# A four-layer graph and mixer network on one NeuronCore: the next layer's tables in two halves, and a nine-tap convolution among the experts' tiles

## The chip, the core and the metric

The kernel runs on one NeuronCore of a Trainium2 chip. The core has five engines that run side by side, each its own instruction queue in a fixed order: TensorE (matrix products and transposes, into PSUM, which has eight banks), VectorE, ScalarE, GpSimd and SyncE, which here only issues DMAs. The metric is the device time of one execution in microseconds.

## The reference, cut to what matters

There are 1250 nodes with 512 features and 21250 edges, all in float32. Each of four layers adds a graph convolution and an attention to `x`, and then a mixture of experts. The change touches three of these parts. In layer 0 it is GATv2, three layers in a row:

```python
for k in range(3):
    xl = x @ Wl[k] + bl[k]
    xr = x @ Wr[k] + br[k]
    m = leaky_relu(xl[src2] + xr[dst2] + ea2 @ We[k], 0.2)
    alpha = segment_softmax(m @ att[k], dst2, n)
    out = segment_sum(xl[src2] * alpha[:, None], dst2) + b_out[k]
    x = relu(layernorm(out + x) * gamma[k] + beta[k])
```

In layer 2 it is the graph convolution with four bases and eight heads, and the experts:

```python
agg = segment_sum((x @ W_bases)[src] * norm[:, None], dst).reshape(n, 4, 64)
weightings = (x @ W_comb + b_comb).reshape(n, 8, 4)
out = einsum('nhb,nbf->nhf', weightings, agg).reshape(n, 512) + conv_bias + x @ W_res + b_res
out = relu(layernorm(out) * gamma + beta)
...
logits = conv1d(gelu(conv1d(xt, rc_w1)), rc_w2)      # three taps each, 512 -> 512 -> 10
gates = softmax over the two largest of 10 logits
y = sum over the two chosen experts of gate * (elu(x @ e_w1) @ e_w2)      # 512 -> 256 -> 512
sh = conv1d(silu(conv1d(xt, sh_w1)), sh_w2)          # nine taps 512 -> 256, then one tap 256 -> 512
z = layernorm(x + y + sh) * ln_g + ln_b
```

## The kernel before

The nodes lie in ten tiles of 128 rows (`NT`), the last one partly filled. The program is written with a tile framework: it names buffers by pool and tag, and the framework adds the semaphores and orders each engine's instructions at build time. That order is close to the program's, but it isn't the same: an instruction whose data are expected early may stand before others that were written earlier. Only SyncE's (SP's) order is kept as written in the parts under `manual_schedule`.

**GATv2** (`gat_layer`, L1203). A layer walks over 188 tiles of 128 edges (47 groups of four). For each edge tile TensorE selects the target rows from `hl` with a one-hot matrix (L1280, L1281), VectorE adds the gathered source rows (L1293) and forms the logit as a product with an accumulated sum (L1296). Groups of a block are transposed, exponentiated and mixed (L1347). A finished block of 107 nodes is normed and turned. As soon as a tile of 128 nodes is complete, its part of the next layer's tables is made: `gat_tables` (L1154) returns eight steps, four matmuls for `wl` and four for `wr`. They go into the list `late`, from which the walk takes one step every second edge tile, or every edge tile while more than eight wait (L1486). With the fourth matmul of a product come, in the same step, ScalarE's copy out of PSUM and VectorE's part: for `wl` the product with the attention vector, whose sum is the 513th column (`left`, L1172), for `wr` the rest that the rounded copy leaves (`right`, L1180). Then SP stores the table. PSUM is split 3 `mm`, 2 `tp`, 2 `more`, 1 `tab` here; these products use `tab`.

**Layer 2's graph convolution** (`layer2_attn`, L2484). Per node tile: the residual product, the counts `ct` cast to float (`cs`, L2567 through `evac`), ten matmuls of counts with bases, the scaled sum `ag` (L2577, L2580), four products of a weighting with a basis (L2585, VectorE) that GpSimd adds up (L2588), a layer norm and a ReLU. Steps of the layer's attention stand between (`go`). `evac` (L130) takes ScalarE and VectorE in turn, over all its callers.

**Layer 2's feed-forward part** (`layer2_ffn`, L2600). The norm of `x` goes to `z` and, transposed, to `xp`; three sums and differences of neighbouring columns (`form`, L2687) serve a fast three-tap convolution with four products for two outputs. A filter comes in pieces of three taps (`piece`, L2617): three DMAs and three GpSimd sums. Up to five pieces are held. `conv` (L2639) makes the routing convolution (four filters of one piece), whose output gives the logits; `route` finds the experts and scatters the rows of `z` to the table `routed_in` in memory; then `conv` makes the shared nine-tap convolution (two filters of three pieces, 192 matmuls), and ten second products follow (L2780, L2782), added to `z` (L2783). Only then come the experts.

**The experts** (`experts`, L2311): 29 tiles of 128 routed rows. A tile needs its rows `xe` (256 KB) and its expert's weights `w` (1025 KB), both with four buffers and loaded three tiles ahead by SP. TensorE turns the rows and makes the two products, the activation lies between, and ScalarE's queue stores the output.

Of the kernel before, what the change touches and what calls it, by code (L numbers as in the profile page):

```python
# [12 lines left out]
F32 = mybir.dt.float32  # L13
# [10 lines left out]
N = 1250  # L24
# [33 lines left out]
class Net:  # L58
# [1095 lines left out]
    def gat_tables(self, L, p, t, xT, bank):  # L1154
# [7 lines left out]
        def product(name, c):  # L1162
            def f():
                if c == 0:
                    d[name] = bank()
                nc.tensor.matmul(d[name], lhsT=xT(c), rhs=L[name][:, c, :], start=c == 0,  # L1166
                                 stop=c == 3)
                if c == 3:
                    (left if name == "wl" else right)(d[name])
            return f  # L1170

        def left(m):  # L1172
            o = p.tile([128, D + 1], F32, tag="tlo", name="tlo")
            nc.scalar.copy(o[:, :D], m)
# [5 lines left out]
        def right(m):  # L1180
            o = p.tile([128, 2, D], F32R, tag="tro", name="tro")
            nc.scalar.copy(o[:, 0, :], m)
# [3 lines left out]
        return [product(name, c) for name in ("wl", "wr") for c in range(4)]  # L1186
# [314 lines left out]
    def run(self, fast):  # L1501
# [4 lines left out]
        with self.tc.tile_pool(name="arm", bufs=1) as self.arm:  # L1506
# [23 lines left out]
            with self.psum():  # L1530
# [36 lines left out]
    def gat_first(self, pv, xtab):  # L1567
        nc, I = self.nc, self.I
        L = self.gat_vectors(0, pv)
        with self.tc.tile_pool(name="l0", bufs=1) as p, \  # L1570
# [3 lines left out]
            with self.tc.tile_pool(name="edge", bufs=1, side="right") as pe, \  # L1574
# [19 lines left out]
                def steps():  # L1594
                    for t in range(NT):
                        for i, f in enumerate(self.gat_tables(
# [3 lines left out]
                            if i % 4 == 3:  # L1600
# [710 lines left out]
    def experts(self, table, n, rowI, act):  # L2311
# [5 lines left out]
        with self.tc.tile_pool(name="ex", bufs=2) as p, \  # L2317
                self.tc.manual_schedule(engines={mybir.EngineType.SP}):
            def load(i):
                xe = p.tile([128, D], F32, tag="xe", name="xe", bufs=4)  # L2320
                nc.sync.dma_start(xe, self.rin[i * 128:(i + 1) * 128, :])
                row = nc.sync.value_load(rowI[0:1, i:i + 1], min_val=0, max_val=(n - 1) * 128)
                w = p.tile([128, 2050], F32, tag="w", name="w", bufs=4)
                nc.sync.dma_start(w, table[bass.ds(row, 128), :])
                return xe, w

            ahead = [load(i) for i in range(3)]
            for i in range(ntiles):
                xe, w = ahead.pop(0)
                if i + 3 < ntiles:  # L2330
                    ahead.append(load(i + 3))
# [16 lines left out]
                nc.scalar.dma_start(self.rout[i * 128:(i + 1) * 128, :], o)  # L2348

# [134 lines left out]
    def layer2_attn(self):  # L2484
        nc, I = self.nc, self.I
        added = self.both_added()
        with self.tc.tile_pool(name="l2", bufs=1) as p:
# [17 lines left out]
            with self.tc.tile_pool(name="egc", bufs=2) as tmp, \  # L2505
# [55 lines left out]
                for t in range(NT):  # L2561
# [5 lines left out]
                    self.evac(cs, ct)  # L2567
                    go()
                    y = self.mm([128, parts * 256])
                    for s in range(NT):  # L2570
# [6 lines left out]
                    nc.vector.tensor_scalar(af, y[:, :256], dinv[:, t:t + 1], None,  # L2577
                                            op0=ALU.mult)
# [4 lines left out]
                    for b in range(4):  # L2583
                        m = tmp.tile([128, 8, 64], F32, tag="m", name="m")
                        nc.vector.tensor_tensor(  # L2585
                            m, wt[:, :, b:b + 1].to_broadcast([128, 8, 64]),
                            ag[:, b:b + 1, :].to_broadcast([128, 8, 64]), op=ALU.mult)
# [11 lines left out]

    def layer2_ffn(self):  # L2600
        nc, I = self.nc, self.I
        keep = self.begin_tail("l2t")
        with self.tc.tile_pool(name="l2f", bufs=1) as p, ExitStack() as right:
# [5 lines left out]
            with ExitStack() as es:  # L2609
# [5 lines left out]
                G = {}  # L2615

                def piece(src, f, j):  # L2617

                    g = cp.tile([128, 4, 4, 128], F32, tag="cw", name="cw", bufs=5)
                    g1 = cp.tile([128, 4, 128], F32, tag="g1", name="g1")  # L2620
                    for i, dst in ((0, g[:, 0]), (2, g[:, 3]), (1, g1)):
                        k = 4 * (3 * j + i)
                        nc.sync.dma_start(dst, src[f][:, k:k + 4, :])
                    nc.gpsimd.tensor_tensor(g[:, 1], g[:, 0], g[:, 3], op=ALU.add)
                    nc.gpsimd.tensor_tensor(g[:, 2], g[:, 1], g1, op=ALU.subtract)
                    nc.gpsimd.tensor_tensor(g[:, 1], g[:, 1], g1, op=ALU.add)  # L2626
                    G[src.tensor.name, f, j] = g

                rc1, sh1 = I["L2_ffn_rc_w1p"], I["L2_ffn_sh_w1p"]
                order = [(rc1, f, 0) for f in range(4)] + [(sh1, f, j) for f in range(2)  # L2630
# [541 lines left out]
```

## Time and profile before

| what | time |
|---|---|
| runs without a profile, median of three | 4537.75 us (4534.72 to 4541.73) |
| the profiled execution as timed | 4585.94 us |
| its span, first to last instruction | 4584.0 us |
| TensorE's mean granted clock | 0.931 of full speed |
| GATv2, three layers, in the span | about 322 to 1620 us |
| layer 2's graph convolution | about 3240 to 3395 us |
| norm, forms and routing convolution | about 3395 to 3511 us |
| routing and shared convolution, second products | about 3511 to 3652 us |
| experts of layer 2 | about 3652 to 3811 us |

The profile is one execution on the chip. A busy share is the time in which an engine works on an instruction, over the length of the stretch asked for. A row of the form `DVE junk L1176 <- ACT tlo L1174` says that VectorE stood still before an instruction of line 1176, and that ScalarE's instruction of line 1174 ended that wait; then come the total in us, the number of times and the longest. A float32 matmul leaves two records. The chain of work that ended last covers only the last experts of layer 3 in this profile, so the stages here are read from busy time by stretch and from the waits.

### The profile page before, as it was taken

Reading aid. Unit: us, or ns where it says so; the run is one execution under the profiler, and the core shown is the slowest. Engines: PE = TensorE matmul, PEld = TensorE weight load, DVE = VectorE, ACT = ScalarE, POOL = GpSimd, SP = SyncE. Lnnn points to the kernel's source line nnn. Section 1 sums busy time; section 2 is a strip of 40 time slices with the busy share of each in tenths; the row PEclk is TensorE's granted clock in tenths of the full one; section 3 lists DMA queues with packets and bytes.
Section 4 is the critical chain, followed back from the end, with each engine's and each line's share of the span. In section 5 each row is a group of like instructions: output and inputs, shape, how many; then the busy total and the mean of one; then the engine's idle time right before and its main releaser. Section 6 shows DMA issues by size and latency. Waiting matters only on the chain. (4 is left out here: it accounts for less than half of the span.)

```text
span 4584.0 us, 49281 instructions
## 1 busy us (share of the span) xinstructions
PE 3946.8 (86%) x15451; PEld 2434.6 (53%) x15466; DVE 2706.4 (59%) x6387; ACT 1502.9 (33%) x2738; POOL 1402.3 (31%) x1339
## 2 busy tenths in 40 slices
PE   6988998899788866799999999997969975898796
PEld 3435554555354444444788876564546552454474
DVE  5358784878398865533796767314692136587301
ACT  2213332334133354110364446122221122455121
POOL 2027662766366501102000000103253003676101
PEclk9989998999899978899999999999989997997798
DMA  6446664666466423401421110392012185565695
GB/s 221 150 123 199 184 188 138 192 185 187 130 180 189 145 66 105 121 18 59 147 68 42 44 41 21 140 336 80 12 54 71 69 282 154 162 205 170 244 338 188
DMA packets 283000, 647.57 MB, mean 141 GB/s; under 512 B 61673, under 2 KB 108905, under 8 KB 267322
## 3 DMA queue, kind: packets, MB, share of 16 engines
q1 hardware_dynamic: 169290, 357.13, 23.5%
q0 software_dynamic: 73088, 234.75, 17.9%
q10 hardware_dynamic: 40352, 52.44, 3.4%
q8 instruction: 127, 2.08, 0.2%
q14 instruction: 143, 1.17, 0.1%
HBM read 528.87 MB, written 120.65 MB: 142 GB/s over the span
## 5 line engine op out<-in xcount | busy, mean ns | idle before, releaser
L231 POOL DMA_INDIRECT xl<-xl,srcI x564 | 606.6, 1075 | 309.4 <-issue 137.4
L1347 PE MATMUL more<-xl,wT 128*128 128x512 f32 x1128 | 578.5, 600 | 26.8 <-ACT wT L1337 25.3
L1280 PE MATMUL mm<-hl,oh 121*128 121x512 f32 x564 | 419.6, 744 | 89.7 <-DVE s L1293 29.7
L1293 DVE TENSOR_TENSOR s<-xl,mm 128x512 f32<-128x512 f32 x534 | 355.0, 680 | 99.9 <-PE mm L1281 42.3
L1296 DVE SCALAR_TENSOR_TENSOR junk<-s,att 128x512 f32<-128x512 f32 x534 | 409.8, 767 | 6.2
L2099 PE MATMUL more<-hh,e 128*128 128x259 f32 x1600 | 384.0, 386 | 11.1 <-ACT o L2042 8.9
L2099 PEld LDWEIGHTS more<-hh,e 128*128 128x128 f32 x1600 | 295.0, 191 | 75.6 <-issue 16.0
L171 PE MATMUL mm<-w,xnT 128*128 128x512 f32 x640 | 307.7, 620 | 13.7 <-DVE xnT L136 5.3
L231 POOL DMA_INDIRECT g<-routed_out,getI x60 | 64.7, 1079 | 676.7 <-DMA routed_out<-o 490.0
L231 POOL DMA_INDIRECT hs<-gcn_h,srcI x188 | 215.5, 1146 | 96.5 <-issue 35.9
L1347 PEld LDWEIGHTS more<-xl,wT 128*128 128x128 f32 x1128 | 196.5, 192 | 86.2 <-ACT wT L1337 34.4
L1281 PE MATMUL mm<-hl,oh 121*128 121x512 f32 x564 | 238.2, 422 | 0.0
L1280 PEld LDWEIGHTS mm<-hl,oh 121*128 121x128 f32 x564 | 111.6, 198 | 232.6 <-issue 135.0
L2649 PE MATMUL mm<-form,cw 128*128 128x312 f32 (+1 forms) x640 | 181.2, 445 | 23.9 <-POOL cw L2626 10.5
L171 PEld LDWEIGHTS mm<-w,xnT 128*128 128x128 f32 x640 | 123.8, 198 | 141.6 <-issue 125.2
L2019 ACT ACTIVATE e<-r,hh 128x512 f32<-128x512 f32 (+1 forms) x240 | 154.2, 646 | 132.5 <-PE more L2099 121.5
L1267 ACT ACTIVATE oh<-nb 112x512 fp32r<-112x512 bf16 x141 | 88.5, 629 | 327.4 <-DMA nb<-nbt 232.9
L2925 PE MATMUL more<-hl,oh 128*128 128x512 f32 x376 | 166.3, 545 | 31.0 <-ACT hl L2885 11.2
L1166 PE MATMUL tab<-w,xT 128*128 128x512 f32 x320 | 165.1, 614 | 19.9 <-DVE junk L1176 18.1
L2022 ACT ACTIVATE e<-r,a 128x512 f32<-128x512 f32 (+1 forms) x240 | 152.3, 646 | 69.4 <-DVE e L2024 57.2
L2024 DVE TENSOR_TENSOR e<-e,e 128x512 f32<-128x512 f32 (+1 forms) x240 | 142.0, 598 | 51.5 <-ACT e L2019 45.1
L1281 PEld LDWEIGHTS mm<-hl,oh 121*128 121x128 f32 x564 | 113.1, 201 | 106.9 <-issue 105.4
(623 smaller groups left out, 7748.6 us busy)
## 6 DMA issues: line engine op xcount, KB each, us to landing
w<-L_ffn_Wp SPq DMA_DIRECT2D x64, 1024.0 KB
w<-L_ffn_table SPq DMA_DIRECT2D x56, 1025.0 KB
neg<-ntab SPq DMA_DIRECT2D x80, 320.0 KB
nb<-nbt SPq DMA_DIRECT2D x141, 128.0 KB
hl<-xr SPq DMA_DIRECT2D x36, 448.0 KB
xr<-tro SPq DMA_DIRECT2D x30, 512.0 KB
xe<-routed_in SPq DMA_DIRECT2D x56, 256.0 KB
routed_out<-o ACTq DMA_DIRECT2D x56, 256.0 KB
```

The source lines that it names most:

```text
L171: self.nc.tensor.matmul(p, lhsT=xT[:, c, t * 128:(t + 1) * 128], rhs=w[:, c, n0:n0 + n], start=c == 0, stop=c == k - 1)
L231: self.nc.gpsimd.indirect_dma_start(out=out, out_offset=None, in_=table, in_offset=bass.IndirectOffsetOnAxis(ap=idx, axis=0), bounds_check ...
L1166: nc.tensor.matmul(d[name], lhsT=xT(c), rhs=L[name][:, c, :], start=c == 0, stop=c == 3)
L1280: nc.tensor.matmul(m, lhsT=s, rhs=hl[:K, 0, :], start=True, stop=False)
L1281: nc.tensor.matmul(m, lhsT=s, rhs=hl[:K, 1, :], start=False, stop=not on_pe(i))
L1293: nc.vector.tensor_tensor(o, d["xl"][:, j, :D], s, op=ALU.add)
L1296: nc.vector.scalar_tensor_tensor(junk, s, 0.0, L["att"], op0=ALU.max, op1=ALU.mult, accum_out=d["lg"][:, j:j + 1])
L1347: nc.tensor.matmul(B[b]["y"], lhsT=d["wT"][:, j, :], rhs=d["xl"][:, j, :D], start=k == 0 and j == 0, stop=last and j == GE - 1)
L2019: nc.scalar.activation(e1[:, :n], R[q, k, 0][:, :n], AF.Exp, bias=HH[q][:, s, 256:257])
L2099: nc.tensor.matmul(ys[j], lhsT=e[:, j * 128:(j + 1) * 128], rhs=HH[q][:, s, :], start=s == 0, stop=s == NT - 1)
L2649: nc.tensor.matmul(m, lhsT=g[:, which, c, :], rhs=forms[form][:, c, q % 2, q // 2:q // 2 + n], start=j + c == 0, stop=j + 1 == len(gs) and ...
L2925: nc.tensor.matmul(y, lhsT=oh, rhs=hl[:, i], start=i + j == 0 and not (self.fast and k), stop=last and i + j == GE)
```

## The change

It has four parts.

1. `gat_tables` returns ten steps instead of eight: `left` and `right` are steps of their own behind the fourth matmul with its copy. They come out of the list `late` one step, so one or two edge tiles, behind the copy. Where the tables are made in a plain loop (L1600) the yield follows each fifth step.
2. In layer 2's graph convolution ScalarE makes `cs`, the first half of `ag`, and the products of the last two of four bases, as eight copies of 64 columns each with a scale operand. VectorE keeps the first two.
3. In layer 2's feed-forward part the filters' pieces get a pool of their own on the other side of the memory, with three pieces instead of five, and one is asked for at the start. ScalarE makes all ten copies of `xp`. PSUM is split 3 `mm`, 3 `tp`, 2 `more` instead of 4 and 4. The norm's shift `ln_b` is added to `x` later, with the second products.
4. `conv` becomes a generator that stops after every four matmuls. The routing convolution still runs through at once. The shared one (48 steps) goes among the experts' tiles through a call `beside(i)`: ten steps ahead of tile 0, two after each tile, none after tiles 7 to 9, and from tile 23 on the second products, two a tile. Weights and rows of the experts have three buffers in layer 2, weights are loaded ahead of rows, in layer 1 too.

```diff
+++ gat_tables
                 if c == 3:
-                    (left if name == "wl" else right)(d[name])
+                    if name == "wl":
+                        o = p.tile([128, D + 1], F32, tag="tlo", name="tlo")
+                        nc.scalar.copy(o[:, :D], d[name])
+                    else:
+                        o = p.tile([128, 2, D], F32R, tag="tro", name="tro")
+                        nc.scalar.copy(o[:, 0, :], d[name])
+                    d[name] = d[name], o
...
-        return [product(name, c) for name in ("wl", "wr") for c in range(4)]
+        return ([product("wl", c) for c in range(4)] + [left] +
+                [product("wr", c) for c in range(4)] + [right])
+++ layer2_attn
-                    self.evac(cs, ct)
+                    nc.scalar.copy(cs, ct)
...
-                    nc.vector.tensor_scalar(af, y[:, :256], dinv[:, t:t + 1], None,
-                                            op0=ALU.mult)
+                    nc.scalar.activation(af, y[:, :256], AF.Copy, scale=dinv[:, t:t + 1])
...
-                        nc.vector.tensor_tensor(
-                            m, wt[:, :, b:b + 1].to_broadcast([128, 8, 64]),
-                            ag[:, b:b + 1, :].to_broadcast([128, 8, 64]), op=ALU.mult)
+                        if b < 2:
+                            nc.vector.tensor_tensor(
+                                m, wt[:, :, b:b + 1].to_broadcast([128, 8, 64]),
+                                ag[:, b:b + 1, :].to_broadcast([128, 8, 64]), op=ALU.mult)
+                        else:
+                            for h in range(8):
+                                nc.scalar.activation(m[:, h, :], ag[:, b, :], AF.Copy,
+                                                     scale=wt[:, h, b:b + 1])
+++ experts(self, table, n, rowI, act, bufs=4, beside=None)
+            ws = [weights(i) for i in range(bufs - 1)]
+            xes = [tokens(i) for i in range(bufs - 1)]
+            if beside is not None:
+                beside(-1)
             for i in range(ntiles):
-                xe, w = ahead.pop(0)
-                if i + 3 < ntiles:
-                    ahead.append(load(i + 3))
+                xe, w = xes.pop(0), ws.pop(0)
+                if i + bufs - 1 < ntiles:
+                    ws.append(weights(i + bufs - 1))
+                    xes.append(tokens(i + bufs - 1))
...
                 nc.scalar.dma_start(self.rout[i * 128:(i + 1) * 128, :], o)
+                if beside is not None:
+                    beside(i)
+++ begin_convs, new; piece() as before, with these pools
+        cw = self.convs.enter_context(self.tc.tile_pool(name="l2cw", bufs=3, side="right"))
...
+            g1 = cw.tile([128, 4, 128], F32, tag="g1", name="g1", bufs=1)
...
+        def ahead(n=3):
+            while order and len(G) < n:
+                piece(*order.pop(0))
...
+        ahead(1)
+++ layer2_ffn
                                 for c in range(4):
...
+                                if j + 1 < len(gs):
+                                    yield
+
+                        m1 = bank([128, n])
+                        yield from products(m1, 1, 1, 1)
...
-                        self.transpose_tile(xp[:, :, 4 + t * 128:4 + (t + 1) * 128], z[:, t, :])
+                        q = self.tp([128, 4, 128])
+                        for c in range(4):
+                            nc.tensor.transpose(q[:, c, :], z[:, t, c * 128:(c + 1) * 128],
+                                                self.ident)
+                        nc.scalar.copy(xp[:, :, 4 + t * 128:4 + (t + 1) * 128], q)
...
-                        nc.gpsimd.tensor_tensor(self.x[:r, t, :], self.x[:r, t, :], be[:r],
-                                                op=ALU.add)
+                self.ahead()
...
+                def shared():
...
+                        yield from conv(sh1, f, 0, 9, silu, self.more)
...
+                    g = self.piece_tile().rearrange("p i c n -> p i (c n)")
+                    nc.sync.dma_start(g[:, :2], I["L2_ffn_sh_w2T"]
+                                      .rearrange("(k p) n -> p k n", p=128))
...
+                    nc.vector.tensor_tensor(z[:, t, :], z[:, t, :], y, op=ALU.add)
+                    r = rows(t)
+                    nc.gpsimd.tensor_tensor(self.x[:r, t, :], self.x[:r, t, :], g[:r, 3],
+                                            op=ALU.add)
+
+                steps = shared()
+                left = list(range(NT))
+
+                def beside(i):
+
+                    for _ in range(10 if i < 0 else 0 if 7 <= i < 10 else 2):
+                        if next(steps, self) is self and left and i >= 23:
+                            second(left.pop(0))
...
-                self.experts(I["L2_ffn_table"], 10, rowI, elu)
+                self.experts(I["L2_ffn_table"], 10, rowI, elu, 3, beside)
+                for _ in steps:
+                    pass
+                for t in left:
+                    second(t)
+            self.convs.close()
```

The pieces for the second filter are asked for when the generator goes on after its first 24 steps, so after tile 10, and the weights of the second products when it ends.

## The prediction, made before the changed kernel was built or run

> **What bounds the kernel now.** I read the page first (busy shares, then the costliest groups), then busy time by stage, then the waits of each stage in which TensorE has gaps. Times are of the profiled execution: span 4584.0 us, 4585.94 us as timed, against a median of 4537.75 us for the runs without a profile; so a saving worked out here is multiplied by 4537.75/4585.94 = 0.99.
>
> ```profile
> PE 3946.8 (86%) x15451; PEld 2434.6 (53%) x15466; DVE 2706.4 (59%) x6387; ACT 1502.9 (33%) x2738; POOL 1402.3 (31%) x1339
> ...
> 460.00:740.00 280.00, 262.05 (x923) 145.94 (x923) 209.25 (x554) 108.91 (x201) 156.94 (x161) 1.00 0.59 171
> 860.00:1200.00 340.00, 319.67 (x1133) 178.61 (x1132) 261.37 (x676) 132.22 (x244) 195.81 (x202) 1.00 0.60 172
> ...
> 3250.00:3390.00 140.00, 124.33 (x349) 64.69 (x347) 126.05 (x238) 45.28 (x71) 60.24 (x40) 0.96 0.06 19
> 3390.00:3448.00 58.00, 29.18 (x97) 21.05 (x98) 47.02 (x72) 6.71 (x13) 46.26 (x27) 0.71 0.26 84
> ...
> 3557.00:3651.00 94.00, 94.00 (x301) 56.11 (x301) 12.57 (x25) 4.35 (x8) 3.80 (x3) 0.98 0.17 62
> 3651.00:3811.00 160.00, 127.91 (x698) 90.90 (x696) 54.44 (x145) 46.59 (x146) 0.00 (x0) 0.96 0.75 252
> ```
>
> Each stage row gives its length, busy TensorE (PE), weight loads, VectorE (DVE), ScalarE (ACT), GpSimd (POOL), granted clock, DMA share, GB/s. TensorE is the bound overall, and what counts is where it has gaps: 18 and 20 us in the parts of the first two GATv2 layers that also make the next tables; 16 us in layer 2's graph convolution, where VectorE is busy for 90%; 29 us at the hand-over to layer 2's feed-forward part; and 32 us among the experts' tiles. The two last rows belong together: for 94 us the convolution fills TensorE while DMA moves 62 GB/s, then for 160 us the experts' weights run at 252 GB/s and TensorE waits for them.
>
> **GATv2's tables.** Nothing is added but place: 20 deferred VectorE pairs and 20 stores. The waits of the three layers (total, times, longest):
>
> ```profile
> DVE junk L1176 <- ACT tlo L1174: 97.4, 20, 9.1
> ...
> PE tab L1166 <- DVE junk L1176: 18.1, 16, 1.4
> ```
>
> VectorE stands 4.9 us at a time before a table's product because ScalarE's copy is late (ScalarE itself waits for POOL's affine steps), and the logits behind it stand too. TensorE loses 18.1 us directly, since the one `tab` bank is read last by that product. As entries of their own in the list that hands out one step per one or two edge tiles (an edge tile is some 2.2 us: 424 us over 191), `left` and `right` come up to 4.4 us after the copy, so most of the stall goes. The last three tables of each layer are made after the edges, where VectorE is idle anyway: 14 of 20 count. Direct: 18.1 x 14/16 = 16; some 3 us more in the logits' waits; less 5 for `right`, which can now come one tile before the next table takes the bank. **14 us**, between 2 (the gaps go over to the transposed weights `wT`, which stop TensorE for 13.5 us in these layers) and 25. Queued behind a late `left` are the same logits as before; ten list entries instead of eight leave a backlog of two, which the drain takes. The stores stay behind their own product on SP. The first table loop yields as often as before: nothing.
>
> **Layer 2's graph convolution (3250 to 3390).** VectorE loses 20 of 40 products at 1.060 us = 21.2, eight casts `cs` at 0.803 = 6.4, ten `ag` at 0.476 = 4.8; it gains about five `qT` copies (3.4), because the alternating copy helper is no longer called between them. Net 29 us off an engine busy for 126 of 140. ScalarE gets 160 copies of 64 columns with a scale operand, 8 casts (its row for 1251 columns: 1.338 us) and ten `ag` (0.473). Here a rule speaks against the change: by the Trainium skill, "ScalarE: Activation LUTs", What ACT_TABLE_LOAD costs, an activation has a fixed 186 ns and 93 ns for each pointer operand beside 0.833 ns a column, and back-to-back ones overlap by 93 ns: eight pieces are 8 x 0.332 - 7 x 0.093 = 2.0 us (an estimate) where one VectorE product is 0.69 to 1.06. The rows agree on the fixed part: 128 columns 0.302 us, 512 columns 0.622. By the row of 128 alone eight are 2.4 us. So ScalarE goes from 45 to 45 + 20 x 2.0 to 2.4 + 10.7 + 4.7 - 2.9, about 98 to 106 of 140: dearer in sum, and off the engine that is full. But TensorE's gap is only 15.7 us, and ScalarE's bursts of 4 to 5 us stand before the attention's activations. Take **3 us**, from -10 (1 us of new wait per node tile) to 15.
>
> **The hand-over (3390 to 3448).** TensorE's waits there:
>
> ```profile
> PE mm L2649 <- POOL cw L2626: 10.5, 1, 10.5
> ...
> PE tp L160 <- DVE xp L2675: 10.1, 1, 10.1
> ...
> PE mm L2649 <- DVE form L2687: 6.0, 1, 6.0
> ...
> PE mm L2649 <- DVE ev L2737: 3.4, 1, 3.4
> ```
>
> 30 us in all. The first piece is now loaded and summed in a pool that begins earlier, on the other side of memory: the 10.5 should go. Ten additions of the norm's shift leave POOL (1.28 each), among them the end that held `rc` until 3447.1: the 3.4 should go. Five copies of `xp` leave VectorE (3.4 us) and six piece sums leave POOL here. The Trainium skill, "SBUF — State Buffer", SBUF: two separate sides, calls the shared port pair an exclusive lock: a two-input VectorE instruction waits for a whole POOL one. The row: 30 `form` subtractions and additions take 0.687 alone, 1.754 at most, 1.088 on average here. By the lock alone each could wait out a full POOL addition (1.26), 38 us; by the row the contention is 30 x 0.4 = 12, of which I take half away. The transposes' 10.1 is what VectorE still owes; I leave most of it. **18 us**, from 10 to 28. Four PSUM banks become three for these products; a product is four matmuls of 0.53 us and is read within 0.5, so nothing. The same for one buffer of `h`: the next write is 8 us on.
>
> **Convolution and experts (3510 to 3811).** From the logits (3510.6) to the last tile's matmul TensorE holds: nine taps, 192 matmuls of 2 records x 0.265 us = 102; the second products, ten times 2.97 = 30; 29 tiles at 4.41 us (the undisturbed pace of the last tiles) = 128; small ones 3. Sum 263 of 300 us. The wait among the tiles (3651 to 3811):
>
> ```profile
> PE tp L160 <- DMA xe<-routed_in: 27.6, 19, 3.2
> ```
>
> Interleaved, TensorE's work need not wait for the tiles' data. After the change, counting on from the logits: the rows are scattered by +41 (20 x 1.27 after 15.5 us of routing) and the first rows are in at about +46, as before. TensorE has ten of 48 steps (2.1 us each) listed for that time; the order is planned from data that are ready (before, VectorE's `oh` of the last layer ran at 3623, 190 us ahead of its place), so more of the 24 steps that need no new piece may move up. Tiles 0 to 9 with the rest of these 24 steps: 53 to 70 us, DMA at 5.5 us a tile about even with TensorE. Tiles 10 to 28: 19 x 4.1 (the wait for the activation chain inside a tile is covered by steps) + 51 + 30 = 159. Then the second filter's pieces: nine loads, 2.4 MB, issued on SP behind tile 12's weights and rows; at 285 GB/s 1.3 + 0.8 MB to the first piece are 7 us, three POOL sums 3.8, against one tile of 4.4: some 5 us exposed. Total 263 to 280 against 300: 20 to 37. The last pieces (0.8 MB, four issues on SP that stood elsewhere), the ten shift additions on idle POOL, and weights two instead of three tiles ahead (TensorE needs some 8 us a tile, a load 4.6) cost nothing while TensorE is the bound; without that cover the look-ahead would show as up to 10 us. **30 us**, from 10 to 50. Layer 1's experts get their loads reordered too; TensorE is busy for 125.9 of 130 us there: nothing.
>
> **Sum:** 14 + 3 + 18 + 30 = 65, times 0.99 = 64: 4537.75 - 64 = **4474 us**.
>
> **Rivals.** (1) Waits change their name (0.22): tables 2, graph convolution -5, hand-over 14, experts 18: 29 us, 4509. For it: `wT` and the logits already stop TensorE, and ScalarE fills up. Against: the experts' wait is DMA, and DMA was idle just before. (2) All gaps close (0.12): 20 + 10 + 25 + 45 = 100, 4438. For it: nothing else is bound at 95%. Against: the hand-over keeps a serial chain. (3) Slower (0.07): TensorE's order is fixed; a step of the second filter stands before tiles while its piece is in flight, the tile behind it gives back one of only three weight buffers late, and DMA idles. It decides from 65/19 = 3.4 us for each of tiles 10 to 28; at 4.6 us, 22 us slower: 4560. Against: once the pieces are in nothing repeats. (4) No change (0.04): the plan puts the steps back in a block, and ScalarE takes what the rest gives; 4538.
>
> **How the numbers follow.** The forecast has 0.55 (gains of 45 to 90). All parts low give 12 us, all high 118; both at once are unlikely. 4435 to 4522 holds the forecast, nearly all of rival 1 and a third of rival 2: 0.8. Faster 0.55 + 0.22 + 0.12 = 0.89, same 0.04, slower 0.07; 0.2% is 9 us, about what a measurement here can tell.
>
> **What would show it.** `junk` waiting for `tlo` below 30 us; VectorE under 80% in the graph convolution and ScalarE near 100 us; no wait for `cw` at the first convolution product; shared-convolution records between expert tiles, the solid 94 us of convolution gone, and `xe` waits under 10 us. The forecast is wrong if ScalarE's 64-column copies take over 0.35 us apiece, or if convolution products wait for `cw` by tens of us.

## The result, and the profile after

| | before | changed |
|---|---|---|
| runs, median of four | 4539.74 us (4534.72 to 4552.93) | 4479.33 us (4478.38 to 4480.39) |
| span of the profiled execution | 4584.0 us | 4477.7 us |

The ratio is 0.9859, 95% interval 0.9842 to 0.9877: 60 us less, where 64 were forecast. The profiled executions differ by 106 us: the one of before was 46 us longer than the median of its runs, the other is as long as its runs. So the kernel before was profiled a second time (the first experiment: span 4545.2 us), and the stages below are taken from that profile as well. A stage runs from one named instruction to the next, each read from the trace: a GATv2 layer from TensorE's first selection of target rows to that of the next layer (the third to its last mixing product), the graph convolution from its first to its last `m` product, on whichever engine that is made, the hand-over from there to the last logit product of the routing, and the last of the four to the last tile's second product.

| stage, us | before, 1st profile | before, 2nd profile | changed | term forecast | found |
|---|---|---|---|---|---|
| GATv2, first and second layer | 876.0 | 864.3 | 835.0 | 14 | 29 |
| GATv2, third layer (not touched) | 419.4 | 400.9 | 403.1 | 0 | 0 |
| graph convolution, first to last `m` | 138.0 | 140.1 | 136.0 | 3 | 2 to 4 |
| hand-over, last `m` to last logit product | 122.4 | 124.7 | 106.9 | 18 | 15 to 18 |
| shared convolution and experts | 300.5 | 297.0 | 288.8 | 30 | 8 to 12 |
| layer 3's aggregation (not touched) | 301.6 | 285.7 | 283.4 | 0 | 0 |

"Found" is the second profile less the changed kernel's for GATv2 and the span between the two differences for the rest. By the second profile the four terms come to 59 us. So the sum of the forecast is right, and so are its two small terms by these marks; the tables gave twice their term, the experts a third of theirs. The border between graph convolution and hand-over is a matter of choice: in the changed kernel ScalarE's last `m` product ends 5.1 us after VectorE's last. By VectorE's last addition of the graph convolution's output to `x` (L185) the first stage takes 146.2, 148.3 and 142.7 us and the second 114.2, 116.5 and 100.3.

One part that the forecast put at nothing costs something. Layer 1's experts, whose loads are reordered too, take 116.1 to 119.0 us from their first transposes to the last second product in the four profiles with the old order, and 120.2 to 124.5 in the ten with the new one. No run changes this order alone.

The changed kernel's profile, the page's first line and then busy time by stretch (length, then busy TensorE, weight loads, VectorE, ScalarE, GpSimd, granted clock, DMA share, GB/s), in the order of the forecast's rows; the last row is the whole stage of convolution and experts:

```profile
PE 3898.0 (87%) x15451; PEld 2418.5 (54%) x15466; DVE 2701.8 (60%) x6347; ACT 1581.3 (35%) x2932; POOL 1399.7 (31%) x1339
...
440.00:720.00 280.00, 272.60 (x977) 154.61 (x976) 238.28 (x593) 118.41 (x219) 174.91 (x175) 1.00 0.62 182
815.00:1145.00 330.00, 318.90 (x1144) 182.32 (x1143) 281.46 (x707) 137.99 (x256) 213.76 (x215) 0.99 0.63 185
...
3192.00:3329.00 137.00, 122.07 (x353) 62.11 (x351) 108.06 (x215) 94.85 (x244) 54.88 (x39) 0.99 0.05 15
...
3329.00:3369.00 40.00, 18.56 (x75) 14.05 (x76) 39.19 (x60) 6.92 (x15) 15.91 (x11) 0.69 0.23 73
...
3437.00:3725.00 288.00, 255.95 (x1156) 172.33 (x1155) 86.67 (x241) 77.79 (x177) 43.33 (x39) 0.97 0.58 194
```

TensorE stands 7 of 280 and 11 of 330 us where the tables are made, instead of 18 and 20. VectorE is at 79% in the graph convolution instead of 90%, and ScalarE has gone from 45 to 95 us there; TensorE stands 15 us there, about as long as before. The last row has 32 us without TensorE. The same two stages in the second profile of before, graph convolution and then convolution with experts:

```profile
3221.00:3362.00 141.00, 126.97 (x350) 66.52 (x348) 126.03 (x238) 44.64 (x70) 58.84 (x40) 0.94 0.06 18
...
3487.00:3783.00 296.00, 261.27 (x1158) 175.09 (x1158) 82.07 (x239) 56.78 (x163) 23.40 (x23) 0.97 0.51 173
```

There TensorE stands 35 of 296 us. The interleaving has hardly made the standing shorter; it has moved it.

### The profile page after: what moved, and what is told of

Same layout as the page of the kernel before. It is cut to its first block, busy times and chain, and to the rows that moved or that the text cites. A ratio compares the mean times of both kernels' runs of the same rounds, so it can differ in the third digit from the quotient of the medians.

```text
span 4477.7 us, 49489 instructions
## 1 busy us (share of the span) xinstructions
PE 3898.0 (87%) x15451; PEld 2418.5 (54%) x15466; DVE 2701.8 (60%) x6347; ACT 1581.3 (35%) x2932; POOL 1399.7 (31%) x1339
## 3 DMA queue, kind: packets, MB, share of 16 engines
q0 software_dynamic: 73088, 234.75, 18.1%
## 4 chain that ended last, share of the span: by engine, by line
PE 39%; DVE 11%; DMA 6%; issue 4%; ACT 2%; POOL 2%; SPq 0%; POOLq 0%; ACTq 0%; DVEq 0%
PE mm L171 6%; PE mm L179 5%; PE more L2105 5%; PE mm L1968 3%; PE mm L3156 2%; PE mm L776 2%; PE mm L2357 2%; PE mm L2352 2%; PE more L2682 2%; PE mm L2067 1%; PE tp L160 1%; PE mm L2682 1%; DMA xe<-routed_in 1%; DVE junk L1996 1%; PE more L2994 1%
## 5 line engine op out<-in xcount | busy, mean ns | idle before, releaser
L231 POOL DMA_INDIRECT xl<-xl,srcI x564 | 618.9, 1097 | 275.8 <-issue 132.7
L160 PE MATMUL tp<-ident,xn 128*128 128x128 f32 x280 | 50.9, 330 | 133.3 <-DVE rsx L207 42.8
```

Of the source, the lines that this page charges most:

```text
L231: self.nc.gpsimd.indirect_dma_start(out=out, out_offset=None, in_=table, in_offset=bass.IndirectOffsetOnAxis(ap=idx, axis=0), bounds_check ...
```

## The experiments

Kernels of one set ran on one chip, beside runs of the kernel before on that chip. In the first set (experiments 1, 2, 5 and 7) before takes 4546 us, in the others 4600, and the changed kernel is longer there by about as much (4537 us for 4479); so kernels are compared by their ratio to before, and stages that hold gathers only within a set. The changed stages without gathers repeat: the graph convolution took 136.0 to 136.3 us in all nine profiles that have it as changed, and the hand-over 106.9 to 107.0 in the eight of these that have it as changed. Before's repeat less well: 138.0 us three times and 140.1 twice for the graph convolution, 122.4 to 125.2 for the hand-over.

**1. The kernel before, again** (no edit).

> The kernel before, unchanged, profiled a second time. The profile that the prediction was made on is a slow execution: 4586 us against runs of 4535 to 4553, and in it TensorE stands 29 us in the GATv2 layers and 42 us in the last layer for nothing that the trace shows. If that was chance, this profile has a span near 4540 and these unnamed gaps are mostly gone, so that the stage times of the two profiles on hand overstate what the change saved in stages it does not touch (third GATv2 layer 16 us, last layer 18 us). If profiling itself costs the time, the span is again near 4584.

Ratio 0.9999 (0.9984 to 1.0014), span 4545.2 us. The unnamed gaps of TensorE in GATv2 (29 us) are gone (0.0) here, though experiment 10 has them again (25 us in the first two layers); the long one at the start of layer 3 is there again (35.2 and 39.2 us), so it is no chance, and half of the expectation was wrong. The stages that the change doesn't touch are shorter by 18.5 (third GATv2 layer) and 15.9 us (layer 3's aggregation) than in the first profile. So a difference between two single profiles is good to 2 or 3 us for stages without gathers, and to much less for those with them.

**2. The tables alone**: the kernel before with the first part of the change's diff (`gat_tables` and the yield of its plain loop).

> The kernel before with the deferred table steps alone. The prediction's term: 14 us less than before, 4526. What the profile of the changed kernel suggests: the first two GATv2 layers are 41 us shorter than in the slow profile of before, of which some 16 a layer are that profile's own (the untouched third layer lost as much), so 10 to 28 us remain. Under 6 us the gaps went over to other waits (the first rival); over 20 the term was too small.

Ratio 0.9937 (0.9918 to 0.9957), 29 us less than before by the ratio. First two GATv2 layers 837.5 us against 864.3 on the same chip: 27 us. The term was half of what it should have been. The waits of the three layers (total, times, longest), in the second profile of before:

```profile
DVE junk L1176 <- ACT tlo L1174: 97.2, 20, 8.8
...
PE more L1347 <- ACT wT L1337: 27.3, 21, 2.6
...
PE tab L1166 <- DVE junk L1176: 18.3, 16, 1.6
```

and in the changed kernel, where `junk` of the tables is L1182:

```profile
DVE junk L1182 <- ACT tlo L1171: 41.1, 6, 9.3
...
PE more L1353 <- ACT wT L1343: 21.4, 17, 5.5
...
PE tab L1166 <- ACT xT L1415: 7.2, 5, 3.5
...
PE tab L1166 <- DVE junk L1182: 2.8, 2, 1.4
```

The direct wait of the table products is gone (18.3 to 2.8), as forecast. In the first two layers alone the wait for the transposed weights `wT` falls too, from 16.4 to 4.8 us, which the forecast had only as the place where the gain might be lost. A new wait for `xT` takes back 5. In this experiment's own profile the three waits of these layers are 1.4, 2.4 and 5.9 us. In the changed kernel TensorE's gaps in these two layers fall from 88.0 to 66.1 us, and its busy time from 776.1 to 768.4.

**3. Delay or spacing?** Two entries more in the list also spread a table's products over more edge tiles. Here VectorE's parts are back behind their copies, with empty entries in their places:

```diff
                     d[name] = d[name], o
+                    (left if name == "wl" else right)()
             return f
...
-        return ([product("wl", c) for c in range(4)] + [left] +
-                [product("wr", c) for c in range(4)] + [right])
+        return ([product("wl", c) for c in range(4)] + [nothing] +
+                [product("wr", c) for c in range(4)] + [nothing])
```

> The changed kernel with VectorE's two instructions of a table issued again straight behind ScalarE's copy, but with an empty entry in the list where they stood, so that a table's products keep the new spacing over the edge tiles. First two GATv2 layers from first logit to first logit: 864 us in the second profile of before, 835 to 848 in the changed kernel. If the delay of VectorE's part is what counts, this is back at some 864, 20 to 27 us slower than the changed kernel (ratio to before 0.991 to 0.992 instead of 0.986). If the wider spacing counts, it stays at 0.986 to 0.987.

Ratio 0.9905 (0.9891 to 0.992), so 21 us slower than the changed kernel. The first two layers took 871.2 us; in the same set before's code took 882.6 (experiment 10) and the next experiment 849.5. So 11 of 33 us come from the spacing and 22 from the delay on top of it; the untouched third layer differs by 3 us between these three profiles. The delay without the wider spacing was not run. (What the expectation calls a layer's first logit is its first selection of target rows.) The waits of these two layers in the spaced kernel, and then in the kernel with before's tables of the same set, are worth reading:

```profile
DVE junk L1186 <- ACT tlo L1171: 44.3, 15, 8.0
...
PE mm L1290 <- DVE junk L1306: 18.1, 6, 7.3
...
PE more L1357 <- ACT wT L1347: 3.9, 5, 1.4
...
PE tab L1166 <- DVE junk L1186: 1.4, 1, 1.4
```

```profile
DVE junk L1176 <- ACT tlo L1174: 90.1, 19, 9.0
...
PE tab L1166 <- DVE junk L1176: 17.6, 15, 2.1
PE more L1347 <- ACT wT L1337: 15.2, 11, 1.9
...
PE mm L1280 <- DVE junk L1296: 10.8, 4, 5.8
```

Spacing alone ends both the direct wait and the wait for `wT`. But VectorE still stands 44 us before the tables' products, the logits' products (`junk` L1306) queue behind, and TensorE's wait for those rises to 18.1 us: here a wait does change its name. With the left part delayed it is 9.5. TensorE's gaps in the two layers sum to 103, 87.5 and, with the delay, 71.4 us; 25, 16 and 8 us of these have no releaser in the trace, so 8.6 of the last 16 lie in waits that the trace names.

**4. The left part alone delayed.**

```diff
                     d[name] = d[name], o
+                    if name == "wr":
+                        right()
             return f
...
-                [product("wr", c) for c in range(4)] + [right])
+                [product("wr", c) for c in range(4)])
...
-                            if i % 5 == 4:
+                            if i in (4, 8):
                                 yield
```

> The changed kernel with only the left table's VectorE part delayed; the right table's subtraction follows its copy as before. The prediction put the whole gain on the left one (16.9 us of waits of the table products for its product in the second profile of before) and a loss of 5 us on the right one. If so, this is up to 5 us faster than the changed kernel, ratio 0.985 to 0.986. If the right one's delay brings part of the 27 us (VectorE stood 24 us before that subtraction), it is 5 to 12 us slower, 0.987 to 0.989.

Ratio 0.9848 (0.9834 to 0.9862), against 0.986 for the changed kernel; first two layers 849.5 us, the changed kernel again 848.6 in the second set. The right one's delay is worth nothing that can be measured.

**5. The graph convolution's work back on VectorE.**

```diff
-                    nc.scalar.copy(cs, ct)
+                    self.evac(cs, ct)
...
-                    nc.scalar.activation(af, y[:, :256], AF.Copy, scale=dinv[:, t:t + 1])
+                    nc.vector.tensor_scalar(af, y[:, :256], dinv[:, t:t + 1], None,
+                                            op0=ALU.mult)
...
-                        if b < 2:
+                        if b < 4:
```

> The changed kernel with the graph convolution's VectorE work put back on VectorE. Prediction's term: 3 us slower, 4482, with VectorE near 90% of that stage again. By the two profiles (138 us from the first to the last product before, 131 after): 7 us slower, 4486. If the copies on ScalarE cost more than they relieve, it is faster than 4479.

Ratio 0.9901 (0.9882 to 0.9921); stage 140.1 us, as in before and 4.1 more than in the changed kernel. (The 131 us of the expectation end with VectorE's last product, 5.1 us before ScalarE's.) The hand-over behind it takes 112.6 us instead of 106.9, though nothing was edited there: the build orders its instructions otherwise, and TensorE has a wait of 3.0 us for `y` that the changed kernel lacks. Which part of the edit brings that is open. Together it is 9.8 us up to the last logit product. The difference of the ratios is 19 us, by the intervals 7 to 31; the stages are the better measure. The costliest rows of the stage in the changed kernel, ScalarE's pieces first (busy, mean ns, idle before):

```profile
L2606 ACT ACTIVATE m<-ag,comb 128x64 f32<-128x64 f32 x160 | 39.9, 334 | 24.7 <-POOL out L2608 24.7
...
L2601 DVE TENSOR_TENSOR m<-comb,ag 128x512 f32<-128x512 f32 x20 | 16.3, 821 | 0.0
L817 DVE TENSOR_TENSOR q<-q,den 128x512 f32<-128x512 f32 x10 | 15.1, 1512 | 0.0
```

and VectorE's two in the second profile of before:

```profile
L2585 DVE TENSOR_TENSOR m<-comb,ag 128x512 f32<-128x512 f32 x40 | 42.2, 1060 | 2.7 <-POOL out L2588 2.6
L817 DVE TENSOR_TENSOR q<-q,den 128x512 f32<-128x512 f32 x10 | 9.8, 979 | 0.0
```

A piece of 64 columns takes 334 ns, and 160 of them fill 39.9 us, 249 ns apiece, so eight are 2.0 us. The rule of the Trainium skill ("ScalarE: Activation LUTs", What ACT_TABLE_LOAD costs) had given 332 ns and 2.0 us, the row for 128 columns 2.4; the rule was the better guide. VectorE gets back 18 us of the stage (126 to 108), less than the 29 of the sum. GpSimd's additions are as many as before; the `m` products are held up less (1.060 us on average, now 0.821), but `q` L817 more (0.979 to 1.512). That the same additions hold it up is argued. TensorE's gaps in the stage have not shrunk: 14.0 and 13.8 us in the two profiles of before, 14.8 in the changed kernel (11.7 to 14.9 over its nine profiles).

**6. The shift's additions back at the hand-over**, and out of the second products:

```diff
...
                             nc.vector.tensor_tensor(
                                 forms[i][:, :, :, t * 64:(t + 1) * 64], u, v, op=op)
+                        r = rows(t)
+                        nc.gpsimd.tensor_tensor(self.x[:r, t, :], self.x[:r, t, :], be[:r],
+                                                op=ALU.add)
...
-                    r = rows(t)
-                    nc.gpsimd.tensor_tensor(self.x[:r, t, :], self.x[:r, t, :], g[:r, 3],
-                                            op=ALU.add)
```

> The changed kernel with the ten additions of the norm's shift back on GpSimd beside the forms at the hand-over. If the hand-over's gain is mainly that VectorE's form instructions are held up less by GpSimd (1.42 us on average in the second profile of before, 0.93 to 1.0 after), the forms are back above 1.2 us and this is 5 to 10 us slower than the changed kernel. If it comes from the copies moved to ScalarE and the smaller first load, it is within 3 us.

Ratio 0.9869 (0.9844 to 0.9894), not to be told from the changed kernel; the hand-over is, with 114.3 us against 106.9. But the forms are not all that explains it. Durations of the 30 form instructions (shortest, median, longest, in ns) in the second profile of before, then the changed kernel, then this one:

```profile
L2687 DVE TENSOR_TENSOR form<-xp x30: 677/1746/1768, 3373.3 to 3418.6; 128x512 f32<-128x512 f32 x30
```

```profile
L2729 DVE TENSOR_TENSOR form<-xp x30: 675/679/1769, 3338.5 to 3368.1; 128x512 f32<-128x512 f32 x30
```

```profile
L2731 DVE TENSOR_TENSOR form<-xp x30: 673/682/1760, 3371.1 to 3403.8; 128x512 f32<-128x512 f32 x30
```

A form takes 0.68 or 1.75 us and hardly anything between. In these three profiles each of the 41 long ones starts while a GpSimd instruction runs: it runs alone, or it waits that one out. That is the exclusive lock of the Trainium skill ("SBUF — State Buffer", SBUF: two separate sides). 20 of 30 had to wait in the second profile of before, 9 in the changed kernel, 12 here. But their number does not set the length of the stage: in the first profile of before 11 waited, the stretch of the forms, first to last, was 36.3 us instead of 46.0, and the hand-over still took 122.4 us instead of 124.7. The stretch is 33.4 us here and 30.2 in the changed kernel.

The additions of `be` cost in two places here (GpSimd's timeline; then VectorE's last addition of the graph convolution's output, here and in the changed kernel):

```profile
3361.58 14.06 POOL L2734 TENSOR_TENSOR x<-x,be 128x512 f32<-128x512 f32 x9 [2.62 <-DMA be<-L_ffn_ln_b]
3375.60 1.71 POOL L2638 TENSOR_TENSOR cw<-cw 128x512 f32<-128x512 f32 x1
```

```profile
3366.12 1.75 DVE L185 TENSOR_TENSOR x<-x,out 98x512 f32<-98x512 f32 x1
```

```profile
3334.85 0.68 DVE L185 TENSOR_TENSOR x<-x,out 98x512 f32<-98x512 f32 x1
```

They run beside the end of the graph convolution, whose last addition ends 10.6 us after the last `m` instead of 6.6. And nine of them stand in front of the first piece's sums, which begin 7.7 us after its load was issued instead of 3.7. What else made the hand-over shorter, the six piece sums and five `xp` copies that left it or the graph convolution (experiment 5), is not settled: no run puts the sums or the copies back alone.

The same stage of the changed kernel shows what did not happen (TensorE's wait for the first piece's sums; SP's wait ahead of that piece's load in the second profile of before and in the changed kernel; SP's timeline):

```profile
PE mm L2682 <- POOL cw L2639: 13.0, 1, 13.0
```

```profile
SPq L2623 <- DVE x L185: 7.8, 1, 7.8
```

```profile
SPq L2637 <- DVE x L185: 6.2, 1, 6.2
```

```profile
3335.60 0.81 SPq L2637 DMA_DIRECT2D cw<-L_ffn_rc_w1p  x2
```

The first piece, asked for at the start, is loaded 0.1 us after VectorE's last addition of the graph convolution's output, in before (3370.1 after 3369.9) as in the changed kernel (3335.6 after 3335.5). So the load still waits for that addition, as it would if its new place lay where the graph convolution's buffers were; that this is the reason is argued, not shown. TensorE waited 13.0 us for the sums, in the two profiles of before 10.5 and 17.7. A load that really begins earlier wasn't tried.

**7. The convolution in a block** in front of the experts, with the change's pools and three buffers:

```diff
-                self.experts(I["L2_ffn_table"], 10, rowI, elu, 3, beside)
                 for _ in steps:
                     pass
                 for t in left:
                     second(t)
+                self.experts(I["L2_ffn_table"], 10, rowI, elu, 3)
```

> The changed kernel with the shared convolution and the second products back in one block in front of the experts' tiles; pools, banks and three buffers stay. If interleaving is worth the 30 us of the prediction, the time is 4509. If it is worth what the two profiles show from the logits to the last tile (300.5 before, 288.8 after), 12 us, it is 4491. At 4480 or less the interleaving gives nothing.

Ratio 0.9909 (0.9887 to 0.993), 22 us above the changed kernel; stage 322.9 us, 34 above it and 22 to 26 above before. But 15.6 us of that are one wait, for the rows of the fourth tile (TensorE's timeline, then SP's):

```profile
3603.69 1.09 PE L160 MATMUL tp<-ident,xe 128*128 128x128 f32 x4 [15.61 <-DMA xe<-routed_in]
```

```profile
3578.06 0.38 SPq L2927 DMA_DIRECT2D dinv<-dinv  x1
3589.31 0.27 SPq L2930 DMA_DIRECT2D dinvb<-dinv  x1
3589.63 7.92 SPq L2932 DMA_DIRECT2D dinvb<-dinv  x1
3597.82 0.37 SPq L2329 DMA_DIRECT2D w<-L_ffn_table  x1
3598.24 0.43 SPq L2334 DMA_DIRECT2D xe<-routed_in  x1
```

Layer 3 stores a small vector `dinv` and reads it back, and in this kernel the three DMAs for it stand on SP in front of the fourth tile's loads, which could have gone from 3581.9 us, when TensorE was done with the first tile's buffers. In before and in the changed kernel they come behind the last tile's loads (from 3789.1 and 3720.6 us). So of the 34 us some 18 are the interleaving's (an estimate: 34 less 15.6; from the 22 of the ratio it would be 7), and of the 22 to 26 above before only 7 to 10 are left for what the interleaving needs, fewer buffers for pieces, rows and weights.

**8. All of the first filter ahead of tile 0**:

```diff
-                    for _ in range(10 if i < 0 else 0 if 7 <= i < 10 else 2):
+                    for _ in range(24 if i < 0 else 0 if i < 10 else 2):
```

> The changed kernel with all 24 steps of the shared convolution's first filter listed in front of the first tile, none among tiles 0 to 9. In the changed kernel TensorE waits 10 us for the first tokens while 15 us of that filter (68 of 192 records) still lie among tiles 0 to 6. If those 10 us are what the interleaving term lost, this is 7 to 10 us faster. If tiles 0 to 11 are bound by their weights' transfers anyway (6 us a tile with or without steps between), the wait only moves from the head into the tiles and the time stays within 3 us.

Ratio 0.9877 (0.9857 to 0.9898), stage 291.4 us: nothing gained. In the changed kernel TensorE's waits of the stage were

```profile
PE tp L160 <- DMA xe<-routed_in: 20.5, 8, 9.9
...
PE more L2682 <- POOL cw L2640: 5.5, 3, 2.0
...
PE mm L2357 <- DVE hT L2856: 5.1, 4, 2.0
```

and on TensorE's timeline (start, us, what; in brackets the idle time before it and what ended it) they sit at tile 0 and at the second filter's first products:

```profile
3453.33 18.05 PE L2682 MATMUL more<-form,cw 128*128 128x313 f32 x68
3481.33 1.08 PE L160 MATMUL tp<-ident,xe 128*128 128x128 f32 x4 [9.95 <-DMA xe<-routed_in]
...
3562.26 3.95 PE L2682 MATMUL more<-form,cw 128*128 128x313 f32 x14 [1.90 <-POOL cw L2640]
```

Here the 10 us at the head are gone, and the waits among the tiles have taken their place:

```profile
PE tp L160 <- DMA xe<-routed_in: 17.5, 12, 3.1
```

Tile 11 ended 123 us after the logits in the changed kernel and 129 here. From tile 0 to tile 11 a tile takes 6.2 us with the filter's steps between and 5.6 without: DMA sets that pace, and what TensorE does there is free or, if there is nothing to do, lost.

**9. Balanced steps**: the first filter ahead of tile 0, the second filter's pieces asked for right behind tile 2's loads, its steps over tiles 3 to 18, the second products over the rest.

```diff
                             yield
                     self.ahead()
+                    yield
...
-                    for _ in range(10 if i < 0 else 0 if 7 <= i < 10 else 2):
-                        if next(steps, self) is self and left and i >= 23:
+                    n = (24 if i < 0 else i == 0 if i < 3 else 2 - i % 2 if i < 19 else 2 if i in (19, 24) else 1)
+                    for _ in range(n):
+                        if next(steps, self) is self and left and i >= 20:
```

> As hoist24, and the second filter's pieces are asked for behind tile 2's loads instead of tile 12's; its steps are spread over tiles 3 to 18, one or two each, and the second products over tiles 20 to 28, so that every tile from 3 on has 1 to 3 us of other work for TensorE. TensorE's work from the logits is 256 us, and it stands 33 us in the changed kernel. If the standing comes from tiles without work between them while DMA is slower than TensorE, some 12 to 20 us go. If DMA is the bound of the whole stage, or TensorE's planned order puts the filter's steps in front of pieces in flight, nothing is gained or it is slower.

Ratio 0.9822 (0.9801 to 0.9844), 17 us below the changed kernel; the intervals just meet, but the stage leaves no doubt: 274.9 us against 289.8 in the same set. TensorE's waits for rows:

```profile
PE tp L160 <- DMA xe<-routed_in: 7.7, 3, 3.7
```

There is none left for a piece. TensorE is busy for 258 of 275 us. Three things were moved at once; the first filter alone gained nothing (experiment 8), but the early request for the pieces and the even spread were not separated.

**10. Before with three buffers** for the experts' rows and weights in layer 2.

```diff
-            ahead = [load(i) for i in range(3)]
+            ahead = [load(i) for i in range(bufs - 1)]
...
-                self.experts(I["L2_ffn_table"], 10, rowI, elu)
+                self.experts(I["L2_ffn_table"], 10, rowI, elu, 3)
```

> The kernel before with three instead of four buffers for the rows and weights of layer 2's experts, nothing else. The prediction put the smaller look-ahead at up to 10 us where no other work covers it. The changed kernel with its convolution in one block is 23 to 26 us longer from the logits to the last tile than before (322.9 against 297.0 and 300.5): if the buffers are the reason, this one has that stage at 315 to 323 and a ratio of 1.003 to 1.005; if the block's 23 us come from the convolution's three piece buffers or from the loads' order, it stays at 297 to 305 and 1.000 to 1.002.

Ratio 1.0004 (0.9991 to 1.0016), so no more than 7 us; the profiled execution has 312.0 us for the stage, 11 to 15 more than the two profiles of before. The two don't agree, so what three buffers cost is not settled, and neither is how the 7 to 10 us left over in experiment 7 divide between buffers, pieces and the loads' order.

**11. The changed kernel again** (no edit).

> The changed kernel unchanged, beside the experiments on one chip. Expected: ratio to before 0.986 again (0.9859 at first), that is some 60 us less, so that the graph convolution's part (0.9901 without it) is 10 to 19 us and the interleaving (0.9909 as a block) some 22 us. If it comes out at 0.989 or more, those two differences shrink to nothing and the parts do not add up.

Ratio 0.986 (0.9834 to 0.9887): the first result holds in a set in which before takes 4600 us instead of 4540.

**12. Balanced steps and the left part alone**: the diffs of 4 and 9 together.

> The changed kernel with the balanced steps (ratio 0.9822, stage from the logits to the last tile 275 us instead of 289) and the right table's subtraction straight behind its copy (0.9848). If the two add up: 0.981, 20 to 24 us faster than the changed kernel, with that stage at 275 us. If left_alone's 0.0012 is only the spread of its runs, 0.982.

Ratio 0.9814 (0.9793 to 0.9834), stage 272.9 us: some 21 us below the changed kernel and 86 below before, the lowest of all ratios. It can't be told from experiment 9 by these intervals.

## Why the prediction was right, and where its parts were not

- **The bound** was read rightly: TensorE, with gaps in four named stages, and by the second profile these four stages differ by 59 us where the runs differ by 60. The profile that the forecast rests on was longer than the runs by 1%; its factor 0.99 was enough for that, because the terms were made from waits and not from stage lengths.
- **GATv2's tables: 14 us, found 29 (27 alone).** The 18 us of direct waits went, as argued. The step that failed is the sum behind them: 3 us for the logits' waits, less 5 for `right`, with `wT` as the gap that would take over. `right` costs nothing (experiment 4), and the wait for `wT` shrank by 12 us instead of growing. The prediction also took two more entries in the list for free; the wider spacing is worth a third of the gain and is what ends the direct wait, while the delay keeps that gain from going over to the logits (experiment 3).
- **Graph convolution: 3 us, found 2 to 4 in its stage.** ScalarE's load was nearly right (95 us, forecast 98 to 106). But TensorE's gaps there did not shrink (14.8 us), so the term came out and the way to it did not: TensorE's busy time is 121 us instead of 124 and 126, and why is open. The term also leaves out the hand-over, where experiment 5 finds another 5.7 us.
- **Hand-over: 18 us, found 15 to 18, but not by the way described.** The step "the 10.5 should go" failed: the load didn't begin earlier, and TensorE waited 13.0 us. What went is the waiting behind the first products, of which the forecast had named 3.4 us. TensorE's gaps over 1 us were 9.3, 10.5, 6.0 and 3.4 us in the first profile of before and 9.3, 17.7 and 10.6 in the second; 7.8 and 13.0 are left. The contention of the forms was 22 us in the second profile (30 x (1.418 - 0.68)), between the 12 that the forecast took from the row and the 38 by the lock alone.
- **Convolution and experts: 30 us, found 8 to 12.** TensorE's work (263 forecast, 257 found), the rows at +46 (45.5) and 5 us for the second filter's pieces (5.5) all came true. The step that failed is that the waits for rows would nearly vanish. Nothing is left for TensorE in tiles 7 to 11, since the pieces arrive only after tile 12's loads, and DMA sets the pace up to there: 20.5 us of waits for rows, 10 of them at tile 0, and 5 for the activation in the last tiles.
- **Layer 1's experts: nothing, found about 4 us more** (121.4 us on average instead of 117.4).
- **The marks named.** VectorE under 80% in the graph convolution (79) and ScalarE near 100 us (95) came true; "`xe` waits under 10 us" (20.5), "no wait for `cw`" (13.0) and "`junk` below 30 us" (41) were missed.
- The two large errors, +15 for the tables and -20 for the experts, cancel. That the total was right is partly luck.

## What to carry to other kernels

Price a stall by what is queued behind it, not only by the wait that names it: here a wait two steps on gave 12 us beside the 15 of the direct one. Work put among tiles hides nothing by itself; it must be there when the transfers are slower than the engine, so ask for its data before that stretch and spread it evenly. A load that is written earlier begins earlier only if what it waits for is earlier too: look for its releaser on the queue that issues it. And when work moves to another engine, end the stage with that engine's last piece, or the gain is read too high.

## What was not expected of the hardware

The changed graph convolution repeats within 0.3 us (136.0 to 136.3 in nine profiles of several sets); with all of its products on VectorE it took 138.0 or 140.1 us. Stages with GpSimd's gathers spread more: the third GATv2 layer, the same instructions in every kernel here, took 400.9 to 420.6 us, layer 3's aggregation 283.4 to 309.6; within the first set it was 400.9 to 404.3 and 284.5 to 290.6. A two-input VectorE instruction of the forms takes 0.68 us, or 1.75 where it meets GpSimd, with at most two in thirty between, so its mean says how often it met one and not how slow it was.
